# Three of the seven block products of Q and K split once more into seven quarter products, with the extra sums on GpSimd

## The chip, the cores and the metric

One core of a Trainium2 chip. The time is the device time of that core in microseconds (us), the median of several executions. A change of under 2% counts as "within 2%". The record marks each run as fast or slow by its time and by the clock that TensorE was granted.

## The reference, cut to what matters

Two attention blocks over x of 8 images x 512 channels x 1024 positions, all in fp32: group norm, one 1x1 convolution to Q, K and V, attention with 8 heads of 64, a projection, and the residual.

```python
xt = xn.reshape(B, C_, N)
qkv = jnp.einsum('oc,bcn->bon', qkv_w, xt) + qkv_b[None, :, None]
q, k, v = jnp.split(qkv, 3, axis=1)
...
attn = jax.nn.softmax(attn, axis=-1)
out = jnp.einsum('bhij,bhdj->bhdi', attn, v)
out = jnp.einsum('oc,bcn->bon', proj_w, out) + proj_b[None, :, None]
```

Q for one image is a 512x512 matrix times a 512x1024 matrix, K likewise. I call one image in one layer a *unit*; there are 16, worked off one after the other.

## The kernel before

The kernel already computes Q, K, V and the projection O with seven block products in place of eight: both matrices are cut 2x2, sums of blocks are multiplied, and the products are added up again. The three tiles `bx`, `by`, `bz` in PSUM, the memory into which this kernel's matmuls write, hold them; each is of two banks. To *evict* a tile is to read it out of PSUM into SBUF, the working memory; a product that is needed twice is copied out (`p1`) or added (`u2`, `u3`) while the tile goes on.

```python
def blocks(name, left, right, tokens, c11, others, done, u3_in):
    bx, by, bz = apair[0], sbank[0], apair[1]
    ...                                  # products(bank, k, start, stop): block product k
    products(bx, 1, True, False)
    p1 = work(accpool, "acc", "p1")
    nc.scalar.copy(p1, bx)
    done(sums)
    products(by, 6, True, False)
    u2 = work(trpool, "tr", "u2")
    nc.vector.tensor_add(u2, by, p1)
    done(sums)
    products(bx, 2, False, True)
    c11(bx)                              # ScalarE evicts it
    done(sums)
    products(by, 7, False, False)
    u3 = work(*u3_in, "u3")
    nc.vector.tensor_add(u3, by, p1)
    done(sums)
    products(bz, 5, True, False)
    others(1, 1, bz, u3)                 # VectorE evicts it and adds u3
    done(sums)
    products(by, 4, False, True)
    others(1, 0, by, p1)
    done(sums)
    products(bz, 3, False, True)
    others(0, 1, bz, u2)
    done(sums)
```

`done` counts the products of Q (1 to 7), K (8 to 14) and V (15 to 21) and at given numbers issues work left over from the attention of the unit before:

```python
def divide_last():
    divide(CC - 1)                       # VectorE: two SBUF inputs, 128x1024
    for h in range(NH):
        add_bias(CC - 1, h)              # ScalarE: two, each waits for the division
...
return {4: [lambda: reciprocals(CC - 1)], 10: [divide_last], 12: mixing[:2], 14: mixing[2:]}
```

## Time and profile before

| | us |
|---|---|
| median | 3341.2 |
| Q and K of a unit | 48.17 |
| V | 24.17 |
| O of the unit before | 24.13 |
| attention | 110.26 |

The stages of the fourth unit are the stretches of this view of the kernel before. Its columns are the stretch, its length, and for each engine the busy time with the count of instructions, then the granted TensorE clock (1.00 is all of it), the DMA share and GB/s.

```profile
core 0: us, PE busy (x) PEld busy (x) DVE busy (x) ACT busy (x) POOL busy (x), PEclk, DMA share, GB/s
618.20:666.37 48.17, 48.17 (x115) 21.38 (x114) 24.91 (x34) 7.59 (x11) 0.00 (x0) 1.00 0.14 45
666.37:690.54 24.17, 24.17 (x113) 21.28 (x112) 8.58 (x8) 2.02 (x2) 0.00 (x0) 1.00 0.07 22
690.54:714.67 24.13, 24.13 (x58) 10.45 (x56) 15.39 (x21) 1.01 (x1) 0.00 (x0) 1.00 0.41 153
714.67:824.93 110.26, 110.26 (x1034) 49.96 (x1033) 99.10 (x123) 76.59 (x83) 1.98 (x1) 1.00 0.08 21
```

TensorE is busy for the whole of each stretch. The others have room in Q and K (VectorE 24.9 of 48.2), and VectorE has little in attention (99.1 of 110.3).

### The profile page before, as it was taken

The page shows a single profiled execution, that of the slowest core. Times are in us where ns is not written, and L with a number is a line of the kernel's source. Part 1 is how long each engine was busy: PE and PEld are TensorE (multiplying, and loading weights), DVE is VectorE, ACT ScalarE, POOL GpSimd, SP SyncE. Part 2 cuts the span into 40 slices and gives each one's busy share as a digit, 9 for nine tenths or more (in the row PEclk, how much of TensorE's full clock was granted, in tenths as well). Part 3 has the DMA queues.
Part 4 walks back from the last instruction along what each step waited for, and adds up shares of the span by engine and source line. Part 5 has one row for each costly group of instructions (what it writes and reads, how often), then busy time and mean ns, then how long its engine had stood idle before and what let it go on. Part 6 is the DMA issues. An engine that isn't in the chain of part 4 may idle for free.

```text
span 3340.0 us, 51079 instructions
## 1 busy us (share of the span) xinstructions
PE 3315.5 (99%) x21002; PEld 1645.3 (49%) x21002; DVE 2375.6 (71%) x2977; ACT 1393.5 (42%) x1549; POOL 48.1 (1%) x32
## 2 busy tenths in 40 slices
PE   8999999999999999999999999999999999999999
PEld 4445454454544545455554544545445454454533
DVE  4876948769486684867848678585785957859577
ACT  1542706336063360733617235172451724517144
POOL 0000000000000000002000000000000000000000
PEclk9999999999999999999999999999999999999999
DMA  2011010110101102012020111201111011110121
GB/s 78 33 39 58 21 64 27 39 58 22 70 27 33 58 21 76 21 33 96 21 85 25 33 58 28 76 15 33 64 33 64 15 37 60 33 63 15 39 71 47
DMA packets 66844, 149.27 MB, mean 45 GB/s; under 512 B 20784, under 2 KB 21040, under 8 KB 66608
## 3 DMA queue, kind: packets, MB, share of 16 engines
q1 hardware_dynamic: 66608, 145.95, 13.3%
q8 instruction: 169, 2.77, 0.4%
q14 instruction: 67, 0.55, 0.1%
HBM read 110.26 MB, written 34.08 MB: 43 GB/s over the span
## 4 chain that ended last, share of the span: by engine, by line
PE 98%; DVE 1%; issue 0%; DMA 0%; ACT 0%; POOL 0%; SPq 0%; DVEq 0%
PE a L514 26%; PE a L288 26%; PE s L486 25%; PE s L288 19%; PE a L486 1%; PE s L437 0%; PE a L437 0%; DMA xn<-x_dram 0%; DVE acc L533 0%; DVE x L422 0%; DVE stats L184 0%; PE a L196 0%; DVE tr L546 0%; DVE u_o L390 0%; POOL y L216 0%
## 5 line engine op out<-in xcount | busy, mean ns | idle before, releaser
L494 ACT ACTIVATE p<-s 128x1024 f32<-128x1024 f32 x976 | 997.2, 1023 | 816.7 <-PE s L486 761.7
L514 PE MATMUL a<-p,v 64*64 64x512 f32 x8192 | 1101.2, 589 | 0.1
L486 PE MATMUL s<-q,k 64*64 64x512 f32 x7808 | 1059.3, 590 | 1.4 <-DVE v L375 1.4
L533 DVE TENSOR_TENSOR acc<-acc,p 128x1024 f32<-128x1024 f32 x768 | 938.7, 1222 | 88.8 <-ACT p L494 41.4
L514 PEld LDWEIGHTS a<-p,v 64*64 64x64 f32 x8192 | 384.9, 131 | 494.4 <-ACT p L494 349.6
L486 PEld LDWEIGHTS s<-q,k 64*64 64x64 f32 x7808 | 385.8, 133 | 437.1 <-issue 434.6
L288 PE MATMUL a<-xn,w 128*128 128x512 f32 x512 | 234.4, 601 | 4.0 <-DVE xn L244 4.0
L531 DVE TENSOR_TENSOR acc<-p,p 128x1024 f32<-128x1024 f32 x128 | 153.7, 1201 | 12.9 <-ACT p L494 12.9
L288 PEld LDWEIGHTS a<-xn,w 128*128 128x128 f32 x512 | 96.9, 192 | 132.7 <-issue 128.1
L546 DVE STREAM_TRANSPOSE tr<-acc 128x1024 f32<-128x1024 f32 x128 | 158.0, 1234 | 0.0
L556 DVE TENSOR_REDUCE red<-tr 128x32 f32<-128x1024 f32 x128 | 153.9, 1202 | 0.6
L540 DVE TENSOR_TENSOR ao<-a,tmp 128x512 f32<-128x512 f32 x128 | 88.0, 687 | 69.9 <-ACT tmp L539 69.9
L300 ACT COPY p_k<-a 128x1024 f32<-128x1024 f32 x16 | 16.2, 1012 | 255.1 <-PE a L288 255.1
L300 ACT COPY p_o<-a 128x1024 f32<-128x1024 f32 x15 | 15.2, 1012 | 244.2 <-PE a L288 244.2
L288 PE MATMUL a<-w,xn 128*128 128x256 f32 x512 | 115.7, 379 | 0.0
L288 PE MATMUL s<-xn,w 128*128 128x512 f32 x256 | 115.2, 593 | 0.4 <-DVE u_q L304 0.4
L300 ACT COPY p_v<-a 128x1024 f32<-128x1024 f32 x16 | 16.2, 1012 | 237.3 <-PE a L288 221.4
L288 PE MATMUL s<-x_t,s2w 128*128 128x512 f32 x256 | 115.1, 592 | 0.0
L288 PE MATMUL a<-x_t,s1w 128*128 128x512 f32 x256 | 115.1, 592 | 0.0
L288 PE MATMUL s<-x_t,w 128*128 128x512 f32 x256 | 115.1, 592 | 0.0
L288 PE MATMUL a<-xn,s4w 128*128 128x512 f32 x256 | 115.1, 592 | 0.0
L288 PE MATMUL a<-ao,wproj_wproj 128*128 128x512 f32 x240 | 107.9, 592 | 0.0
(129 smaller groups left out, 2843.4 us busy)
## 6 DMA issues: line engine op xcount, KB each, us to landing
rb<-drec SPq DMA_DIRECT2D x128, 256.0 KB, 3.9
xn<-mid SPq DMA_DIRECT2D x36, 512.0 KB, 5.0
xn<-x_dram SPq DMA_DIRECT2D x32, 512.0 KB, 5.1
x<-x_dram SPq DMA_DIRECT2D x32, 512.0 KB, 4.6
mid<-x SPq DMA_DIRECT2D x64, 256.0 KB, 2.1
x<-mid SPq DMA_DIRECT2D x28, 512.0 KB, 4.6
out_dram<-x SPq DMA_DIRECT2D x56, 256.0 KB, 2.1
w<-qkv_wT_dram SPq DMA_DIRECT2D x6, 1024.0 KB, 11.2
```

The costliest lines, as they stand in the source:

```text
L288: nc.tensor.matmul(dst, at[:, c, ts(i, P)], moving[:, c, :], start=start and c == 0 and not (tokens and i % 2), stop=stop and c == 1, skip ...
L300: nc.scalar.copy(p1, bx)
L486: nc.tensor.matmul(bank[e * H : (e + 1) * H, j, :], w.k[pr][j * H : (j + 1) * H, t * P + e * H : t * P + (e + 1) * H], w.q[pr][j * H : (j ...
L494: exp = nc.scalar.activation(p, bank, AF.Exp, scale=SCALE)
L514: nc.tensor.matmul(banks[r][j * H : (j + 1) * H, :], w.v[rows, t, lo : lo + D], p[rows, j, :], start=(t == 0), stop=(t == NT - 1),)
L531: nc.vector.tensor_add(acc, state["first"], p)
L533: nc.vector.tensor_add(acc, acc, p)
L540: i1 = nc.vector.tensor_add(w.ao[pr // 2][:, pr % 2, ts(qh, FD)], banks[1], tmp)
L546: nc.vector.transpose(tr, state["acc"].pop(c))
L556: nc.vector.tensor_reduce(red[:, :, qh, :], state["tr"].rearrange("p j (f i) -> p j f i", i=BL), AX.X, ALU.add)
```

## The change

The intent: split products 2, 4 and 3 of Q and of K once more, so that each takes seven calls of 128x128 on 256 columns. Before it took four on 512 columns (3.43 us from start to start in the kernel before), which last as long as eight on 256 (3.45 us in its V). The price is more sums. ScalarE copies the partial results out, GpSimd adds them, and GpSimd also makes the mixed quarter blocks. The quarter blocks of the weights are mixed once a layer, in its first unit. To make room in SBUF, the accumulator of attention and the transpose buffer go from two buffers to one. The diff, cut to its core:

```diff
-    accpool = pool("accpool", 2)
+    accpool = pool("accpool", 1)
-    trpool = pool("trpool", 2)
+    trpool = pool("trpool", 1)
+    def mix_inner(name, right):              # four GpSimd adds of 256 columns, for 2, 4 and 3
+        t = ppool.tile([P, 4, FD2], F32, tag="p", name=f"{name}_t")
+        ...
+        def inner_products(k, bank, more):
+            left, right = inner[k]
+            one, two = sbank[1][:, 0, :FD2], (bz if k == 2 else bx)[:, 0, :FD2]
+            product(1, one, True, False)
+            nc.scalar.copy(rest[:, 0, :FD2], one)
+            product(2, bank[:, 0, :FD2], False, True)
+            product(3, bank[:, 0, FD2:], False, True)
+            product(6, one, False, False)
+            nc.scalar.copy(rest[:, 0, FD2:], one)
+            product(4, bank[:, 1, :FD2], False, True)
+            product(5, two, True, True)
+            nc.scalar.copy(rest[:, 1, FD2:], two)
+            nc.gpsimd.tensor_add(rest[:, 0, FD2:], rest[:, 0, FD2:], rest[:, 1, FD2:])
+            product(7, one, False, True)
+            nc.scalar.copy(rest[:, 1, :FD2], one)
+            nc.gpsimd.tensor_add(rest[:, 1, FD2:], rest[:, 1, :FD2], rest[:, 1, FD2:])
+            if more is not None:
+                nc.gpsimd.tensor_add(more, more, rest)
-        products(bx, 2, False, True)
-        c11(bx)
+            c11(bx, inner_products(2, bx, None))     # now on VectorE, as the others are
-        products(by, 4, False, True)
+            inner_products(4, by, p1)
-        products(bz, 3, False, True)
+            inner_products(3, bz, u2)
-        return {4: [...], 10: [divide_last], 12: mixing[:2], 14: mixing[2:]}
+        return {4: [...], 9: [divide_last], 15: [partial(mix, 0)], 17: [partial(mix, 1)]}
```

I call the products inside a quartered product its *parts*, 1 to 7.

More of the change, by code (lines that the diff above doesn't have):

```diff
@@ L165, in mix_right, with mix_inner_left @@
         return {1: b11, 2: b21, 3: b22, 4: t4, 5: t1, 6: t2, 7: b12}, parts
+    INNER = (2, 4, 3)
+    def mix_inner(name, right):
+        gp = nc.gpsimd
+        b11, b12 = right[:, 0, :FD2], right[:, 0, FD2:]
+        b21, b22 = right[:, 1, :FD2], right[:, 1, FD2:]
+        t = ppool.tile([P, 4, FD2], F32, tag="p", name=f"{name}_t")
+        t1, t2, t3, t4 = (t[:, i, :] for i in range(4))
+        parts = [
+            partial(gp.tensor_sub, t1, b12, b11), partial(gp.tensor_sub, t2, b22, t1),
+            partial(gp.tensor_sub, t3, b22, b12), partial(gp.tensor_sub, t4, b21, t2),
+        ]
+        return {1: b11, 2: b21, 3: b22, 4: t4, 5: t1, 6: t2, 7: t3}, parts
+    def mix_inner_left(name, tag, left):
+        gp = nc.gpsimd
+        a11, a12 = left[:, 0, :P], left[:, 1, :P]
+        a21, a22 = left[:, 0, P:], left[:, 1, P:]
+        t = wpool.tile([P, 3, P], F32, tag=tag, name=name)
+        s1, s2, s4 = (t[:, i, :] for i in range(3))
+        parts = [
+            partial(gp.tensor_add, s1, a21, a22), partial(gp.tensor_sub, s2, s1, a11),
+            partial(gp.tensor_sub, a21, a11, a21), partial(gp.tensor_sub, s4, a12, s2),
+        ]
+        return {1: a11, 2: a12, 3: s4, 4: a22, 5: s1, 6: s2, 7: a21}, parts
     def load_proj(l, tag):
@@ L269, in fast_path, with blocks @@
         pass
-    def blocks(name, left, right, tokens, c11, others, done, u3_in):
+    def blocks(name, left, right, tokens, c11, others, done, u3_in, inner=None):
         bx, by, bz = apair[0], sbank[0], apair[1]
@@ L292, in products, with product @@
                     )
+        def inner_products(k, bank, more):
+            left, right = inner[k]
+            one, two = sbank[1][:, 0, :FD2], (bz if k == 2 else bx)[:, 0, :FD2]
+            rest = tpool.tile([P, 2, FD], F32, tag=f"o{k if k != 3 else 1}", name=f"m{k}_{name}")
+            def product(j, dst, start, stop):
+                nc.tensor.matmul(
+                    dst, left[j], right[j], start=start, stop=stop, skip_group_check=True
+                )
+            product(1, one, True, False)
[13 more added lines that the diff above has]
+                nc.gpsimd.tensor_add(more, more, rest)
+            return rest
         def work(pool, tag, k):
@@ L305, in blocks @@
         done(sums)
-        products(bx, 2, False, True)
-        c11(bx)
+        if inner:
+            c11(bx, inner_products(2, bx, None))
+        else:
+            products(bx, 2, False, True)
+            c11(bx)
         done(sums)
@@ L315, in blocks @@
         done(sums)
-        products(by, 4, False, True)
+        if inner:
+            inner_products(4, by, p1)
+        else:
+            products(by, 4, False, True)
         others(1, 0, by, p1)
         done(sums)
-        products(bz, 3, False, True)
+        if inner:
+            inner_products(3, bz, u2)
+        else:
+            products(bz, 3, False, True)
         others(0, 1, bz, u2)
@@ L340, in projections, with c11 @@
             ]
-            def c11(bank):
-                for i in range(2):
-                    w.last[sel].append(
-                        nc.scalar.activation(
-                            tiles[i][:, :FD], bank[:, i, :], AF.Identity,
-                            bias=vec[:, l, bias, i : i + 1],
-                        )
-                    )
+            def c11(bank, more):
+                others(0, 0, bank, more)
             def others(r, h, bank, more):
@@ L361, in projections @@
             left = w.lefts["qk".index(sel)]
-            blocks(f"{sel}_{u}", left, w.right, False, c11, others, done, (ppool, "p"))
+            blocks(f"{sel}_{u}", left, w.right, False, c11, others, done, (ppool, "p"), w.inner[sel])
             setattr(w, sel, tiles)
@@ L642, in divide_last, with mix @@
                 add_bias(CC - 1, h)
-        w.right_o, mixing = mix_right(f"o_{u}", *w.ao)
-        return {4: [lambda: reciprocals(CC - 1)], 10: [divide_last], 12: mixing[:2], 14: mixing[2:]}
+        mixing = []
+        def mix(i):
+            if not mixing:
+                w.right_o, parts = mix_right(f"o_{u}", *w.ao)
+                mixing.extend(parts)
+            for part in mixing[2 * i : 2 * i + 2]:
+                part()
+        return {
+            4: [lambda: reciprocals(CC - 1)], 9: [divide_last], 15: [partial(mix, 0)],
+            17: [partial(mix, 1)],
+        }
     xn = load_xn(0)
@@ L661, in fast_path @@
     rest[12] = mixing_o
+    inner_left = {}
     old = None
@@ L670, in fast_path @@
         if u == B + 1:
-            rest[16] = mixing_o
+            rest[18] = mixing_o
+        inner_right, inner_parts = {}, {"q": [], "k": []}
+        for k in INNER:
+            if u % B == 0:
+                for i, sel in enumerate("qk"):
+                    inner_left[sel, k], parts = mix_inner_left(
+                        f"l{k}{sel}_{u}", f"l{k}{sel}", lefts[i][k]
+                    )
+                    inner_parts[sel] += parts
+            inner_right[k], parts = mix_inner(f"r{k}_{u}", right[k])
+            inner_parts["q"] += parts
+        w.inner = {
+            sel: {k: (inner_left[sel, k], inner_right[k]) for k in INNER} for sel in "qk"
+        }
+        for g, sel in ((1 if u == 0 else 0, "q"), (7, "k")):
+            rest[g] = [*rest.get(g, ()), *inner_parts[sel]]
+        for part in rest.get(0, ()):
+            part()
         projections(w, rest)
@@ L742, in verdict @@
         nc.vector.tensor_mul(both, low[:, 0:1], low[:, 1:2])
-    project_last(old, [part for g in (4, 10) for part in rest[g]] + [verdict])
+    project_last(old, [part for g in (4, 9) for part in rest[g]] + [verdict])
     nc.tensor.matmul(turns[0][:1, :1], both, ones[:, :1], start=True, stop=True)
```

## The prediction

> **What bounds the kernel now.** I read the page first: busy shares, slices, chain.
>
> ```profile
> PE 3315.5 (99%) x21002; PEld 1645.3 (49%) x21002; DVE 2375.6 (71%) x2977; ACT 1393.5 (42%) x1549; POOL 48.1 (1%) x32
> PE 98%; DVE 1%; issue 0%; DMA 0%; ACT 0%; POOL 0%; SPq 0%; DVEq 0%
> ```
>
> TensorE is busy 99% and is 98% of the chain that ended last; the first slice alone is not full. So each us of matmul removed is a us of the kernel, and each us that TensorE is made to wait is a us lost: nothing absorbs it. GpSimd is idle.
>
> Second, the timeline of one unit (one image in one layer; 16 of them, 206.7 us apart). At the start of Q, TensorE, then ScalarE, then VectorE:
>
> ```profile
> 411.46 3.70 PE L288 MATMUL a<-xn,w 128*128 128x512 f32 x8
> 415.00 3.60 PE L288 MATMUL s<-x_t,s2w 128*128 128x512 f32 x8
> 418.44 3.60 PE L288 MATMUL a<-xn,w 128*128 128x512 f32 x8
> ...
> 415.20 1.01 ACT L300 COPY p_q<-a 128x1024 f32<-128x1024 f32 x1 [1.79 <-PE a L288]
> ...
> 411.91 2.55 DVE L533 TENSOR_TENSOR acc<-acc,p 128x1024 f32<-128x1024 f32 x2
> 414.38 0.68 DVE L540 TENSOR_TENSOR ao<-a,tmp 128x512 f32<-128x512 f32 x1
> 414.98 1.23 DVE L546 STREAM_TRANSPOSE tr<-acc 128x1024 f32<-128x1024 f32 x1
> 416.25 1.22 DVE L556 TENSOR_REDUCE red<-tr 128x32 f32<-128x1024 f32 x1
> 417.39 1.22 DVE L669 TENSOR_TENSOR x_t<-xn,x_t 128x1024 f32<-128x1024 f32 x1
> 418.52 1.22 DVE L669 TENSOR_TENSOR xn<-xn 128x1024 f32<-128x1024 f32 x1
> 419.65 1.22 DVE L304 TENSOR_TENSOR u_q<-s,p_q 128x1024 f32<-128x1024 f32 x1
> ```
>
> A block product starts every 3.43 us: four calls of 128x512, each two records (x8). VectorE comes out of attention backlogged, with no gap; u_q ends at 420.9, and the product that overwrites its bank is due at 421.87: one us of slack.
>
> Third, V, whose calls have the 256 columns that the change will use, and the middle of K:
>
> ```profile
> 459.64 3.62 PE L288 MATMUL a<-w,xn 128*128 128x256 f32 x16
> 463.09 3.62 PE L288 MATMUL s<-s2w,x_t 128*128 128x256 f32 x16
> ...
> 463.34 1.01 ACT L300 COPY p_v<-a 128x1024 f32<-128x1024 f32 x1 [14.76 <-PE a L288]
> ...
> 442.74 1.23 DVE L304 TENSOR_TENSOR u_k<-s,p_k 128x1024 f32<-128x1024 f32 x1 [5.53 <-PE s L288]
> 443.88 1.22 DVE L596 SCALAR_TENSOR_TENSOR ao<-ao,rb 128x1024 f32<-128x1024 f32 x1
> 445.02 0.08 DVE L596 DVE_READ_ACCUMULATOR ao<-ao,rb 128x1 f32 x1
> 446.10 1.26 ACT L345 ACTIVATE k<-a,vec 128x512 f32<-128x512 f32 x2 [5.86 <-PE a L288]
> 447.26 1.33 ACT L603 ACTIVATE ao<-ao,vec 128x512 f32<-128x512 f32 x2
> ```
>
> Eight 256-column calls also take 3.45 us, so one takes 0.43. The copy starts 0.25 us after the next product has begun. Then, for how fast TensorE resumes after a wait, the start of attention, and for GpSimd beside VectorE the one place where both work:
>
> ```profile
> 508.04 1.29 DVE L422 TENSOR_TENSOR x<-a,u_o 128x512 f32<-128x512 f32 x2 [0.95 <-PE a L288]
> 509.45 0.41 PEld L486 LDWEIGHTS a<-q,k 64*64 64x64 f32 x8 [0.45 <-DVE x L422]
> 509.70 1.04 PE L486 MATMUL a<-q,k 64*64 64x512 f32 x8
> ...
> 1531.00 1.27 POOL L688 TENSOR_TENSOR w<-w 128x512 f32<-128x512 f32 x1
> 1532.23 1.26 POOL L688 TENSOR_TENSOR s4w<-w,s2w 128x512 f32<-128x512 f32 x1
> ...
> 1532.66 3.05 DVE L390 SCALAR_TENSOR_TENSOR u_o<-x,vec,u_o 128x512 f32<-128x512 f32 x2
> ```
>
> The wait sits on the weight load: read done at 509.33, load at 509.45, matmul at 509.70, so 0.37 us from the reader's end to the matmul.
>
> [...]
> 1. [...] The trace has 1.23 us between starts for 512. [...]
> 2. [...] the pair above took 3.05 us beside GpSimd, 1.41 elsewhere, 0.8 more for each.
> [...]
>
> **The change part by part.**
> Removed: each of products 2, 4, 3 of Q and K becomes seven calls of 256 columns in place of eight. Saved 0.43 us, times 6 a unit, 2.57 us; times 16, **41 us**. That is all there is to gain, 1.2%.
>
> Added on the path: inside a quartered product one PSUM area holds parts 1, 1+6 and 1+6+7, and ScalarE copies it between. A copy of 128x256: from 0.58 us for 512 columns and 1.01 for 1024, 0.84 ns a column, so 0.37. A round trip from the end of a matmul to the next one in that area: 0.23 + 0.37 + 0.37 = 0.97 us.
> - Parts 6 and 7 each have two calls, 0.86 us, ahead of them as cover: 0.11 short, 12 times a unit, 1.3 us.
> - Product 3 follows product 4 at once, and its part 1 overwrites the area that part 7 of product 4 has just filled: no cover. 0.97 us, twice a unit, 1.9.
> - The block after (K, then V) begins in the bank that held part 5 of product 3; only part 7 (0.43) covers it: 0.54, twice, 1.1.
>
> Together **4.3 us a unit**, already more than the 2.57 saved.
>
> Moved: the last division and its two bias adds go from after K's product 2 to before it. ScalarE then holds the two bias adds ahead of the copies that K's product 2 needs, and they wait for the division. On the times above: product 6 of K ends at 442.47; u_k, then the division until 445.1; biases 445.2 to 446.5; small copy until 446.9; matmul at 447.2. It was due 1.29 us (three calls) after 442.47, at 443.8. **3.4 us a unit**, in 15 units.
>
> Start of a unit: twelve GpSimd adds of 256 columns[...]. The first four meet VectorE's last sums and the division, two SBUF inputs each: at some 0.5 us (the 0.8 scaled to the shorter adds) for three, VectorE is 1.5 us late, u_q ends near 422.5. TensorE would want the bank at 421.4 plus the waits above; I count 1.0. With one accumulator buffer, p_q can't be copied before the transpose is done (417.7), so it ends at 418.8 in place of 416.2, just when product 2 needs the bank: 0.4. The other eight adds wait for x_t, near 420.1,[...]; the parts of Q's product 2 queue behind them[...]. Sum **2.3 us a unit**, the softest term.
>
> Off the path: [...] VectorE takes over two evictions of 0.75 from ScalarE. The single transpose buffer costs nothing[...]. Moving the mixing into V costs nothing; V's VectorE has gaps of 2 to 5 us.
>
> Sum for 14 ordinary units: 4.3 + 3.4 + 2.3 - 2.6 = 7.4, 104 us. First unit: no division, about 4. First unit of layer 1: also 24 adds of 128 columns, twelve ahead of Q's[...]. Total +119: 3341.9 + 119, about **3460 us**.
>
> **The rivals.**
> - *All waits hidden*: TensorE shows only the 41 us, 3301. For it: [...] GpSimd idles. Against: the round trip in one PSUM area is three durations from the trace with no cover in two places a unit.
> - *Round trips only*: bias adds and start of unit cost nothing, because something orders ScalarE otherwise than I read. Then 3342 + 16 x 1.7, 3369, within 2%. Against: in K above the bias adds keep program order.
> - *GpSimd becomes the bound*: if small adds carry a large fixed cost (say 1.2 us for 256), each partial sum comes 3 us later and its evictions hold VectorE; products 4 of Q and K then wait too, 3 us more a unit and above 3500. For it: only one size was measured; its power op on 128x4 takes 1.98.
> - *The buffers bind*: the single accumulator delays the copy by far more than 0.4. Then the start costs 4 or 5 us, 3500.
>
> **Range and chances.** The firm part, 4.3 + 3.4 - 2.6, gives +78 or so, 3420; dropping a third of each gives 3395. The soft terms doubled give 3500. 8 in 10: 3395 to 3505. Slower by over 2% means above 3408.7, which the firm part alone passes: 0.80. Within 2%: 0.17, if the bias adds do not block. Faster by over 2%: 0.03, since more than the 41 us would have to come.
>
> **What would show it.** Busy time of TensorE's Q and K groups lower by 41 us; 128x256 copies near 0.37 us; weight loads in the new products waiting for ScalarE's copies, near 1 us at product 3, near 3.4 at K's product 2; the bias adds ahead of K's small copies; sums at a unit's start above 1.22 us[...]. Wrong would be a unit spacing under 208.4 us, or waits mostly for GpSimd.

Cut from it are a list with a length for GpSimd's adds of 256 columns, which no trace of this case had shown, and what rests on that length. Two terms of the sum are among this: the last of three at a unit's start (0.9 us, beside the 1.0 and 0.4 that still stand; together the 2.3), and 4 us in the first unit of layer 1. The sum, +119 us and 3460, has both in it; without them it comes to about +101 (119 less 16 times 0.9 and less 4), 3442. The firm part, +78, does not contain them.

What is left of the list is from the rows above it: GpSimd's adds of 512 columns start 1.23 us apart, and VectorE's pair beside them took 3.05 us where it takes 1.41 elsewhere. The 0.5 us for the shorter adds is my estimate from the 0.8 of that pair. That ScalarE keeps the order of the program is read from K: the division ends at 445.10 and ScalarE is idle until 446.10, and yet the bias adds come after the eviction that starts there, at 447.26.

## The result, and the profile after

| | before | after |
|---|---|---|
| median, us | 3341.2 (6 runs) | 3432.7 (6 runs) |
| Q and K, all units | 774.0 | 861.6 |
| V, all units | 388.2 | 390.0 |
| O | 361.9 | 361.9 |
| attention | 1765.0 | 1766.8 |

The ratio is 1.0278 (95% interval 1.0265 to 1.0292): slower. Ratios here are the mean time of one kernel's fast runs over that of the other's fast runs of the same rounds, so they are not quite the ratio of the medians. The stages are told from the starts of the matmuls in the two traces. Nearly all of the 91.5 us came into Q and K.

The page of the kernel after, busy shares and the chain that ended last by engine:

```profile
PE 3324.7 (97%) x21578; PEld 1798.3 (52%) x21578; DVE 2449.6 (71%) x3041; ACT 1497.8 (44%) x1869; POOL 565.5 (16%) x528
...
PE 80%; DVE 9%; issue 6%; POOL 3%; ACT 2%; DMA 0%; DVEq 0%; POOLq 0%; SPq 0%; ACTq 0%
```

TensorE is no longer the whole chain: a fifth of it runs through VectorE, GpSimd, ScalarE and issue. That is a chain followed back from the end, not time lost; much of it ran beside matmuls. Its busy time is up, 3324.7 us from 3315.5, although it has less to do. Matmuls held at half their clock are a part of this, and not the larger: the first stretch below has the full clock (1.00), and its busy time is 47.67 us where e11, the last experiment, with the waits gone, has 45.70. Around each wait some 0.16 us of the last call's modelled end (0.59 us, where the next call follows at 0.43) and 0.11 us of a slower first call (0.70 us in place of 0.59) count as busy too. The same four stretches of the fourth unit as above:

```profile
637.13:689.63 52.50, 47.67 (x150) 27.44 (x148) 25.66 (x34) 13.72 (x30) 25.45 (x25) 1.00 0.11 31
689.63:713.91 24.28, 24.28 (x113) 21.43 (x113) 12.25 (x12) 2.40 (x3) 4.00 (x4) 1.00 0.14 44
713.91:738.03 24.12, 24.12 (x57) 10.48 (x55) 15.39 (x21) 1.01 (x1) 0.00 (x0) 1.00 0.41 153
738.03:848.41 110.38, 110.38 (x1033) 53.34 (x1032) 99.15 (x123) 76.52 (x83) 3.65 (x2) 1.00 0.07 21
```

Q and K take 52.50 us in place of 48.17, and TensorE is idle for 4.83 of them. Who held it is in the view of waits, here of the weight loads of TensorE, at which this trace shows its waits: us in all, times, longest.

```profile
PEld s L331 <- ACT m_k L336: 48.7, 15, 3.4
...
PEld s L331 <- DVE u_q L372: 17.9, 16, 5.5
PEld s L317 <- DVE u_q L362: 16.5, 15, 1.1
...
PEld s L331 <- ACT m_q L346: 14.1, 16, 1.2
PEld s L331 <- ACT m_k L346: 13.8, 16, 0.9
...
PEld a L317 <- ACT m_q L343: 6.9, 16, 0.4
PEld a L317 <- ACT m_k L343: 6.9, 16, 0.4
PEld a L331 <- ACT p_q L358: 6.8, 15, 2.2
```

In the timeline of that unit the weight loads are idle 0.24 us between matmuls of 512 columns with no wait (0.19 us of load in each 0.43), so a row can be too large by some 0.2 us for each time. I took the loss from the starts of the matmuls: how much later one begins than 0.215 us (256 columns) or 0.429 us (512) after the one before. Those sums are what is quoted from here on.

The largest, in K of the fourth unit. TensorE, then ScalarE, then VectorE in the timeline of the kernel after:

```profile
670.53 0.60 PE L331 MATMUL a<-xn,l2k 128*128 128x256 f32 x2
673.97 0.70 PE L331 MATMUL s<-r_t,l2k 128*128 128x256 f32 x2 [2.84 <-ACT m_k L336]
...
672.33 1.33 ACT L664 ACTIVATE ao<-ao,vec 128x512 f32<-128x512 f32 x2 [4.83 <-DVE ao L657]
673.57 0.35 ACT L336 COPY m_k<-s 128x256 f32<-128x256 f32 x1
...
669.93 1.22 DVE L362 TENSOR_TENSOR u_k<-s,p_k 128x1024 f32<-128x1024 f32 x1 [1.64 <-PE s L317]
671.07 1.22 DVE L657 SCALAR_TENSOR_TENSOR ao<-ao,rb 128x1024 f32<-128x1024 f32 x1
```

Part 6 of K's product 2 needs ScalarE's copy of part 1 (`m_k`). The copy stands behind the two bias adds, these wait for the division, and the division for `u_k`. TensorE stands still for 3.0 us, in 15 units.

And the end of Q in the same timeline, product 4 into product 3 (the same line 331 for all parts):

```profile
658.32 0.59 PE L331 MATMUL s<-r_t,w 128*128 128x256 f32 x2
659.38 0.70 PE L331 MATMUL s<-xn,s4w 128*128 128x256 f32 x2 [0.46 <-ACT m_q L346]
...
658.96 0.37 ACT L346 COPY m_q<-s 128x256 f32<-128x256 f32 x1
```

Part 1 of product 3 overwrites what part 7 of product 4 left, so it starts only when that is copied: 0.05 us after the copy's end, and 0.63 late.

### The profile page after: what moved, and what is told of

Read it like the earlier page. It is cut to its first block, busy times and chain, and to the rows that moved or that the text cites. A ratio compares the mean times of both kernels' runs of the same rounds, so it can differ in the third digit from the quotient of the medians.

```text
span 3431.1 us, 53597 instructions
## 1 busy us (share of the span) xinstructions
PE 3324.7 (97%) x21578; PEld 1798.3 (52%) x21578; DVE 2449.6 (71%) x3041; ACT 1497.8 (44%) x1869; POOL 565.5 (16%) x528
## 3 DMA queue, kind: packets, MB, share of 16 engines
HBM read 110.26 MB, written 34.08 MB: 42 GB/s over the span
## 4 chain that ended last, share of the span: by engine, by line
PE 80%; DVE 9%; issue 6%; POOL 3%; ACT 2%; DMA 0%; DVEq 0%; POOLq 0%; SPq 0%; ACTq 0%
PE s L547 21%; PE a L575 21%; PE a L317 16%; PE s L317 13%; DVE acc L594 5%; PE s L331 5%; PE a L331 3%; POOL r_t L762 2%; PE a L547 1%; DVE ao L657 1%; DVE tr L607 1%; ACT ao L664 1%; DVE u_q L372 1%; DVE acc L592 1%; ACT p L555 1%
## 5 line engine op out<-in xcount | busy, mean ns | idle before, releaser
L575 PE MATMUL a<-p,v 64*64 64x512 f32 x8192 | 1116.2, 589 | 0.1
L547 PE MATMUL s<-q,k 64*64 64x512 f32 x7808 | 1074.7, 590 | 1.4 <-DVE v L436 1.4
L575 PEld LDWEIGHTS a<-p,v 64*64 64x64 f32 x8192 | 400.0, 132 | 479.2 <-ACT p L555 338.8
L547 PEld LDWEIGHTS s<-q,k 64*64 64x64 f32 x7808 | 415.6, 133 | 407.7 <-issue 405.2
L762 POOL TENSOR_TENSOR r_t<-xn 128x256 f32<-128x256 f32 x60 | 74.0, 1233 | 1196.7 <-PE a L575 1196.7
L244 POOL TENSOR_TENSOR y<-var,half 128x4 f32<-128x4 f32 x16 | 32.2, 2015 | 1006.1 <-DVE var L242 1006.1
L664 ACT ACTIVATE ao<-ao,vec 128x512 f32<-128x512 f32 x128 | 88.3, 713 | 98.6 <-DVE ao L657 98.6
L317 PE MATMUL a<-xn,w 128*128 128x512 f32 x256 | 120.2, 613 | 4.8 <-DVE xn L272 4.4
L317 PEld LDWEIGHTS a<-w,xn 128*128 128x128 f32 x512 | 96.1, 190 | 19.1 <-ACT m_k L343 6.9
L266 ACT ACTIVATE xn<-xn,shift,scale 128x512 f32<-128x512 f32 x124 | 99.5, 805 | 7.1 <-DVE shift L262 7.1
```

Of the source, the lines that this page charges most:

```text
L266: nc.scalar.activation(cols, cols, AF.Identity, bias=st["shift"][:, c : c + 1], scale=st["scale"][:, c : c + 1],)
L317: nc.tensor.matmul(dst, at[:, c, ts(i, P)], moving[:, c, :], start=start and c == 0 and not (tokens and i % 2), stop=stop and c == 1, skip ...
L547: nc.tensor.matmul(bank[e * H : (e + 1) * H, j, :], w.k[pr][j * H : (j + 1) * H, t * P + e * H : t * P + (e + 1) * H], w.q[pr][j * H : (j ...
L575: nc.tensor.matmul(banks[r][j * H : (j + 1) * H, :], w.v[rows, t, lo : lo + D], p[rows, j, :], start=(t == 0), stop=(t == NT - 1),)
L664: nc.scalar.activation(cols, cols, AF.Identity, bias=vec[:, units[u][0], VB, pr : pr + 1])
L762: part()
```

## The experiments

Eleven kernels ran. The first four are the changed kernel with one thing undone or altered, and the old kernel with one part of the change; their rounds shared the runs of the kernel before, 3341 us.

**1. The bias adds after product 2.** The division stays at 9.

```diff
-            divide(CC - 1)
-            for h in range(NH):
-                add_bias(CC - 1, h)
+            divide(CC - 1)
+        def bias_last():
+            for h in range(NH):
+                add_bias(CC - 1, h)
-            4: [...], 9: [divide_last], 15: ...
+            4: [...], 9: [divide_last], 10: [bias_last], 15: ...
```

> The changed kernel with one thing moved: the two bias adds that follow the last division are issued after K's product 2 and not before it (the division itself stays). My theory ([...] the bias adds hold the small copies that K's quartered product 2 needs): the wait of 3.0 us, 15 times, goes, 45 us, and with it most of the stretches in which TensorE was granted half its clock, some 8 more: 3380 us. Rival (GpSimd's sums set the pace of K): nothing moves, 3433.

Measured: 3373.2 us, ratio 1.0098 (1.0081 to 1.0114). The change loses 59.5 of its 91.5 us by the place of two instructions. The wait of 3.0 us is gone from the trace, and so is every stretch at half the clock except those at the start and the end (granted clock of the profiled run 0.998, in the change 0.994). The rival falls.

**2. Other PSUM areas, first try.** Product 3's partial sums go to the second bank of the score tile.

```diff
             one, two = sbank[1][:, 0, :FD2], (bz if k == 2 else bx)[:, 0, :FD2]
+            if k == 3:
+                one, two = sbank[1][:, 1, :FD2], sbank[1][:, 0, :FD2]
```

> The changed kernel with other PSUM areas for product 3: its partial sums go to the second bank of the pair and its part 5 to the first, so that nothing is overwritten that ScalarE is about to copy. My theory (round trips through one area): the waits between product 4 and product 3 (24 us in the trace) and before the next block (8 us) go: 3401 us. Rival (product 3 waits for GpSimd or for its evictions): under 5 us gained.

Measured: 3464.7 us, ratio 1.0369 (1.0352 to 1.0386), slower than the change itself. Both theories missed, because the edit did not do what it was meant to. TensorE and ScalarE in the timeline of this kernel:

```profile
663.73 0.59 PE L333 MATMUL s<-r_t,w 128*128 128x256 f32 x2
664.78 0.70 PE L333 MATMUL s<-xn,s4w 128*128 128x256 f32 x2 [0.46 <-ACT m_q L348]
...
667.24 0.70 PE L333 MATMUL s<-r_t,l3q 128*128 128x256 f32 x2
668.40 0.70 PE L333 MATMUL s<-r_t,s4w 128*128 128x256 f32 x2 [0.46 <-ACT m_q L345]
...
664.36 0.37 ACT L348 COPY m_q<-s 128x256 f32<-128x256 f32 x1
...
667.98 0.37 ACT L345 COPY m_q<-s 128x256 f32<-128x256 f32 x1 [0.79 <-PE s L333]
```

The matmul at 664.78 now writes the other bank and still waits for the copy that ends at 664.73. And part 7 (668.40) waits for the copy of part 5 (ends 668.35), which is in the other bank too: a new wait of 0.63 us, 32 times. The dependences of this program are kept for the two-bank tile as a whole. Of the round trips, only the wait before the next block (0.30 us) is gone from this trace, because part 5 is no longer in that block's bank. For the wait into product 3 the run neither supports nor refutes the theory; experiment 5 does it properly.

**3. Eight of the twelve GpSimd adds later.** The mixed quarter blocks for products 4 and 3 are made after product 2's sums.

```diff
-            inner_parts["q"] += parts
+            if k == 2:
+                inner_parts["q"] += parts
+            else:
+                later += parts
...
+        rest[3] = [*later, *rest.get(3, ())]
```

> The changed kernel with the eight GpSimd adds for products 4 and 3 of a unit issued after product 2's sums in place of before them. My theory (product 2's sums queue behind twelve adds, so Q's second sum u3 is late and product 4 waits for it): the 16 us of that wait go, those of the first units of both layers too: 3417 us. Rival (the adds are needed where they were; late ones make products 4 and 3 wait): slower than 3433.

Measured: 3424.2 us, ratio 1.0253 (1.0236 to 1.0270). Q's product 4 no longer waits for `u_q`: the 16 us are gone from the trace. The time fell by only 8.5, because this kernel's trace has more stretches at half the clock, 13 of 3.4 us between start and end in place of 8 (granted clock of the profiled run 0.993, in the change 0.994). They follow the wait in K, which is still there. (What such a stretch costs is under "right or wrong" below.)

**4. The old kernel with the single buffers.** Only the two pool sizes.

> The kernel before with only the single buffers for the accumulator and the transpose. My theory ([...] only the first copy of Q waits for the transpose, about 1 us, and that is covered): 3341 to 3344 us. Rival (the single buffer is what makes the start of a unit wait): 10 us or more slower.

Measured: 3343.3 us, ratio 1.0007 (0.9990 to 1.0024). Single buffers by themselves cost nothing in the time that can be told from noise. In the trace the attention of an ordinary unit takes 110.38 us, as in the change, where the kernel before has 110.26: most of the change's 2 us in attention come from here. They can still matter where something else is late, which the next ones show.

**5. Other PSUM areas, second try.** Product 4 and product 3 use two different tiles in turn, and part 5 comes third, so that its copy is long done when its area is needed.

```diff
-            one, two = sbank[1][:, 0, :FD2], (bz if k == 2 else bx)[:, 0, :FD2]
+            one, two = {2: (sbank[1], bz), 4: (bx, sbank[1]), 3: (sbank[1], bx)}[k]
+            one, two = one[:, 0, :FD2], two[:, 0, :FD2]
             product(1, ...); product(2, ...)
+            product(5, two, True, True)
+            nc.scalar.copy(rest[:, 1, FD2:], two)
             product(6, ...); product(3, ...); product(4, ...)
-            product(5, two, True, True)
-            nc.scalar.copy(rest[:, 1, FD2:], two)
             product(7, ...)
```

> The second try at the PSUM areas. The first put both areas into the two banks of one tile, and every wait there was for the tile as a whole, so it tested nothing but added waits. Now product 4 keeps its partial sums in the first tile (bx) and its part 5 in the score tile, product 3 the other way round, and part 5 comes third. My theory (round trips through one area): the waits between product 4 and product 3 (20 and 3.4 us) and before the next block (6.2 and 1.7) go, 31 us: 3401 us. Rival (product 3 waits for evictions or for GpSimd anyway): under 5 us gained.

Measured: 3403.1 us, ratio 1.0186 (1.0169 to 1.0203; whether over 2% is unclear), 29.6 us faster than the change. The waits into product 3 and into the next block are not in its trace any more. The theory of the round trips holds.

**6. No GpSimd adds at a unit's start.** The quarter products take unmixed blocks.

```diff
-        return {1: b11, 2: b21, 3: b22, 4: t4, 5: t1, 6: t2, 7: t3}, parts
+        return {1: b11, 2: b21, 3: b22, 4: b21, 5: b12, 6: b22, 7: b11}, []
```

> The changed kernel without the twelve GpSimd adds of a unit's start; the quarter products take unmixed blocks, so the result is wrong on purpose, with the same matmuls and copies. My theory (those adds read SBUF beside VectorE's two-input instructions and delay them, and the sums of product 2 queue behind them): VectorE's division and last sums are back at 1.22 us, the waits for u_q (13.7 and 4.0), for p_q (4.8) and for Q's u3 (16) go, some 36 us: 3397 us. Rival 1 (only the queue on GpSimd matters[...]): 16 us, 3417. Rival 2 (the single buffers are what makes the start wait): nothing at the start moves, 3417 too, with u_q and p_q waiting as before.

Measured: 10858 us, and the result correct. The wrong Q and K failed the kernel's own check of its sums, so that after its fast part the program ran its general path, which computes all again. The whole time says nothing, but the trace holds the fast part, which ends at 3399.0 us with the matmul that makes the flag (3424.8 in the change). That is 26 us, not the 36 expected; this trace also has more stretches at half the clock in its middle, 13 in place of 8. In it the waits for `p_q` and for Q's `u3` are gone, and of `u_q`'s wait one is left. VectorE and TensorE at the start of the fourth unit:

```profile
629.18 1.23 DVE L594 TENSOR_TENSOR acc<-acc,p 128x1024 f32<-128x1024 f32 x1
...
635.59 1.22 DVE L362 TENSOR_TENSOR u_q<-s,p_q 128x1024 f32<-128x1024 f32 x1
...
637.18 3.60 PE L317 MATMUL s<-xn,w 128*128 128x512 f32 x8
```

The last sum takes 1.23 us; in the change two of them take 3.40. `u_q` is ready at 636.81, before the product that needs its bank. The single buffers are still single here, so rival 2 falls, and rival 1 too, since more than the queue went away.

**7. Three edits together** (1, 3 and 5).

> The changed kernel with three of the edits at once: bias adds after product 2, the new areas and order of parts, the adds for products 4 and 3 after product 2's sums. If the waits are independent: 3373 - 31 - 15 = 3327 us, with the waits for u_q and p_q at a unit's start left, some 20 us. Rival (removing one wait brings out another of about the same size, since VectorE and GpSimd are the real limit of Q and K): 3350 or more, slower than the kernel before.

Measured: 3323.9 us, ratio 0.9949 (0.9932 to 0.9965). The waits are independent ones: none came up in place of those removed, and 3433 is now 3324. Alone, the three edits gained 59.5, 29.6 and 8.5 us, 98 together; the other 11 us go with the stretches at half the clock, which e3 and e5 still had (granted clock 0.993 and 0.994) and this trace has only at the start and the end (1.000). The kernel is half a per cent faster than the one before, which is within 2%. What is left in its trace is the start of a unit: 13.7 and 1.7 us for `u_q`, 3.2 and 1.6 for `p_q`. Product 3 now follows product 4 without a gap (TensorE, fourth unit):

```profile
635.98 0.59 PE L332 MATMUL a<-r_t,w 128*128 128x256 f32 x2
636.41 0.59 PE L332 MATMUL s<-xn,s4w 128*128 128x256 f32 x2
```

**8. In addition, two of VectorE's four mixing instructions earlier.**

```diff
-        for part in mixing[2:]:
+        for part in mixing[2 if u == 0 else 4 :]:
...
-            elif c == 2 + CC and t in (2, 5):
-                mixing[int(t == 5)]()
+            elif c == 2 + CC and t in (2, 5, 6, 7):
+                mixing[(2, 5, 6, 7).index(t)]()
```

> e7 with the last two of VectorE's four mixing instructions moved from a unit's start into the attention before it. My theory: VectorE has 2.3 us less of backlog when Q begins, so neither u_q nor p_q makes TensorE wait: 3310 us, about 1% faster than the kernel before, 3301 being the limit of the saved matmuls. Rival (VectorE is full in attention, so the two push the exponentials out): attention longer by over 1 us a unit and no gain over e7.

Measured: 3342.1 us, ratio 1.0005 (0.9988 to 1.0021). My theory was right on Q and K and wrong on the sum: Q and K fell from 46.87 to 45.99 us a unit, and attention rose from 110.38 to 112.38. The rival holds. ScalarE in this kernel's attention:

```profile
614.10 1.94 ACT L556 ACTIVATE p<-s 128x1024 f32<-128x1024 f32 x2 [2.95 <-DVE acc L593]
```

The exponential waits 2.95 us for VectorE's sum, which frees its buffer. TensorE in turn waits for such an exponential 14 times, 24.6 us in all. VectorE at 90% had no 2.3 us to spare there.

**9. Unused tiles to shift the buffers.** Two tiles are taken from the pool and never touched, so that the first mixed block would get the buffer of a later exponential and GpSimd would start later.

```diff
+        for i in range(2):
+            ppool.tile([P, N], F32, tag="p", name=f"skip{i}_{u}")
```

> e7 with two unused tiles taken from the pool first, so that the first GpSimd tile of a unit gets the buffer of the last but one exponential and its four adds can start only when VectorE is done with all but its last sum. My theory (the four adds hold up VectorE's division and sums, each by some 0.5 us, and nothing else): division and sums back at 1.22 us, the waits for u_q (13.7 and 1.7) and p_q (3.2 and 1.6) gone, 20 us: 3304 us, 1.1% faster than the kernel before. Rival (the adds are then too late for product 2's third part): no gain over e7, 3324, with a wait for GpSimd in its place.

Measured: 3324.0 us, ratio 0.9948 (0.9934 to 0.9962), the same as e7. The edit did not take: GpSimd's first add of the fourth unit starts at 613.68 us, and at 613.76 in e7. It seems that tiles which nobody touches took no buffer. Nothing is learned about the theory.

**10. Division and bias adds both behind product 2, as in the kernel before.**

```diff
-            4: [...], 9: [divide_last], 15: ...
+            4: [...], 10: [divide_last], 15: ...
```

> The changed kernel with the division and its bias adds both back behind product 2, as in the kernel before. My theory: as e1, 3373 us, since VectorE has slack there. Rival (the division was moved because behind product 2's evictions, which wait for GpSimd, it makes u_k late): slower than e1 by 10 us or more, with a wait for u_k.

Measured: 3374.6 us, ratio 1.0099 (1.0084 to 1.0115), as e1. Leaving `divide_last` where the kernel before has it would have been right; K's `u_k` shows no wait. ScalarE in K of the fourth unit, where the small copy now goes ahead of the bias adds:

```profile
663.02 0.37 ACT L336 COPY m_k<-s 128x256 f32<-128x256 f32 x1 [2.81 <-PE s L331]
...
669.12 1.33 ACT L664 ACTIVATE ao<-ao,vec 128x512 f32<-128x512 f32 x2 [3.14 <-DVE ao L657]
```

**11. GpSimd's first add after VectorE's last sum.** The edit that e9 meant, as a dependence.

```diff
-                nc.vector.tensor_add(acc, acc, p)
+                w.last_sum = nc.vector.tensor_add(acc, acc, p)
...
+            n = part()
+            if i == 0 and old is not None:
+                tc.add_manual_dep(getattr(n, "ins", n), name_of(old.last_sum), DEP, reason="after the sums")
```

> e7 with the first GpSimd add of a unit made to depend on VectorE's last sum of the attention (e9's unused tiles changed nothing: they took no buffer, and the adds began where they did in e7). Expected as for e9: division and last sums back at 1.22 us, the waits for u_q (13.7 and 1.7) and p_q (3.2 and 1.6) gone, 20 us: 3304 us, 1.1% faster than the kernel before. Rival: the adds are then too late for product 2's third part, and a wait for GpSimd takes the place, 3324.

Measured: 3306.7 us, ratio 0.9894 (0.9878 to 0.9911): 1.1% faster than the kernel before, which is within 2%, with an interval that leaves out 1. It does the same work as the change, with 126 us less. The start of the fourth unit in the kernel after, VectorE and GpSimd:

```profile
636.64 1.75 DVE L657 SCALAR_TENSOR_TENSOR ao<-ao,rb 128x1024 f32<-128x1024 f32 x1
...
638.32 3.40 DVE L594 TENSOR_TENSOR acc<-acc,p 128x1024 f32<-128x1024 f32 x2
...
635.53 1.78 POOL L762 TENSOR_TENSOR r_t<-xn 128x256 f32<-128x256 f32 x1 [80.83 <-PE a L575]
637.39 1.59 POOL L762 TENSOR_TENSOR r_t<-xn,r_t 128x256 f32<-128x256 f32 x1
```

and in e11:

```profile
611.23 1.22 DVE L658 SCALAR_TENSOR_TENSOR ao<-ao,rb 128x1024 f32<-128x1024 f32 x1
...
612.37 2.55 DVE L595 TENSOR_TENSOR acc<-acc,p 128x1024 f32<-128x1024 f32 x2
...
615.06 0.72 POOL L769 TENSOR_TENSOR r_t<-xn 128x256 f32<-128x256 f32 x1 [85.77 <-DVE acc L595]
615.86 0.73 POOL L769 TENSOR_TENSOR r_t<-xn,r_t 128x256 f32<-128x256 f32 x1
```

Beside each other, the division takes 1.75 us in place of 1.22, two sums 3.40 in place of 2.55, and GpSimd's adds over twice their time. One after the other, both are back at their own, and GpSimd, started 3.8 us after the division's start in place of 1.1 before it, has its four adds done 6.7 us after the division's start in place of 5.7. So the delay costs it about one us, and that one us was free but in one unit, the ninth, where TensorE waited 0.7 us for such an add.

## Why the prediction was right or wrong

It was right in direction and size: slower, 3460 forecast and 3432.7 measured, inside the range. Of the +119 us forecast, +91.5 came. Term by term, all units together; the measured ones are the late starts of matmuls in the trace of the kernel after:

| term | forecast, us | measured, us |
|---|---|---|
| matmuls saved | -41 | -40 |
| no cover for parts 6 and 7 | 21 | 0 |
| product 4 into product 3 | 31 | 24 |
| last part 5 before the next block | 17 | 10 |
| bias adds ahead of K's copies | 51 | 47 |
| start of a unit | 37 | 38 |
| TensorE at half its clock | not foreseen | 9 |
| sum, and the first units | 119 | 88 |

The forecasts are the per-unit terms times 16, or 15 for the bias adds; 14 of the 37 us at the start of a unit, and 4 us in the last line, are the terms cut. The last line has 3 us more for what I gave the first unit of each layer beyond them. The measured sum lacks 3 us, of which attention has 2. The 40 are from e11, where the waits are gone: a unit's Q and K take 45.70 us in place of 48.17, 2.47 times 16.

But for one term, the waits, the queues that hold them and the order of their sizes were as forecast. One of the signs asked for did not show: TensorE's busy time in Q and K of the fourth unit fell by 0.5 us, not by 2.6 (see the page above). e1 and e10 show the bias adds, e5 the two round trips, e3 the queue on GpSimd, e6 and e11 that GpSimd and VectorE hold each other up, and e7 that these are independent.

**The term that failed** is "Parts 6 and 7 each have two calls, 0.86 us, ahead of them as cover: 0.11 short, 12 times a unit, 1.3 us". In the trace the parts of a quartered product follow each other at 0.43 us with no wait. The round trip was mis-sized: I had put 0.37 us from the end of the reading to the next matmul, taken from the start of attention. In the timeline above, part 7 of product 4 starts at 658.32 and holds TensorE until 658.75, the copy runs from 658.96 to 659.33, and the matmul follows at 659.38; the second pass after it comes 0.11 late. That is 0.63 us and 0.11, together 0.74 in place of 0.97. With 0.63 the 0.86 us of cover is enough. The same error makes the next two rows too large: 0.74 in place of 0.97 between products 4 and 3, and 0.30 (0.195 and 0.106) in place of 0.54 before the next block. These three rows differ from the measured ones by 35 us, more than the whole of the error.

**The start of a unit** came out right in all, 38 us for 37, with its parts otherwise mixed: `u_q` 0.97 us (0.86 and 0.11) in 15 units where I had 1.0; `p_q` 0.3 us for 0.4; `u3` 16 us in the trace, of which 8 lie in the first unit of each layer, where twelve more GpSimd adds stand ahead. I had given 0.9 to each unit and 4 to one first unit, the two terms cut above; the other units have 0.57. The remaining 3 us are matmuls at half the clock after the `u3` waits of the two first units. That the sum came out so near is luck.

**What I had not foreseen** is the clock. After the 3.0 us pause in K, the trace has stretches of 3.4 us in which TensorE's granted clock was 0.50, in six of 15 units. The kernel after in the thirteenth unit, timeline of TensorE:

```profile
2584.53 1.22 PE L331 MATMUL s<-r_t,l2k 128*128 128x256 f32 x2 [2.84 <-ACT m_k L336]
2585.54 1.06 PE L331 MATMUL a<-r_t,w 128*128 128x256 f32 x2
2586.40 1.06 PE L331 MATMUL a<-r_t,l2k 128*128 128x256 f32 x2
2587.25 1.06 PE L331 MATMUL s<-r_t,w 128*128 128x256 f32 x2
```

Each row is one call of two passes. They should follow each other at 0.43 us, and they start 0.85 to 1.01 apart. Units with such a stretch after K's pause have Q and K of 53.9 to 55.5 us, where the others have 52.5; over five such units that is 9 us more (the sixth, at the start of layer 1, has other waits too). e1 and e10 have no such stretch in the middle of the program, which explains why e1 gained more than the 47 us of its wait.

Which pauses of the same 3.0 us were followed by one goes, in this trace, with where a pause lies in time. What follows is measured here, from the clock that the trace of the kernel after records and from its matmuls. All its stretches at half the clock begin on one grid of 3.413 us: the first after K's pause at 460.76 us, the next at 1307.27, 248 steps later, another at 2583.86, 622 steps after the first. In the interval 457.35 to 460.76 TensorE stood still for 2.50 us of its pause, and the granted clock was 0.50 from there to 464.17. The pause of the fourth unit was split by a line of the grid, 1.43 us on one side and 1.58 on the other, and the clock stayed at 1.00. The largest part that fell into one interval was 2.33 us or more in five of the 15 units, and half the clock followed in all five; 2.13 or less in eight, and it followed in none; 2.16 in two, and it followed in one of them. So what told these pauses apart was where they fell on the grid. 15 pauses of about one length show no more than that.

## What to carry to other kernels

Where TensorE is the whole chain (98% of it in the kernel before), fewer matmuls pay only if every round trip through another engine has other matmuls ahead of it. Here 0.86 us of them were enough for a round trip of 0.63, and with none TensorE was 0.63 us late: count the calls between a part and the next one in the same tile, and give neighbours different tiles. Before moving an instruction to an earlier place in a program, look at every queue that it passes through, and at what will stand behind it there: two bias adds held a copy, and TensorE for 3.0 us, in 15 units, and cost more here (47 us) than all the quartered products save (40). Work moved to an idle engine is not free where the two engines hold each other up, as GpSimd and VectorE did here (1.75 us in place of 1.22 for the division, 1.6 to 1.8 in place of 0.72 for GpSimd's adds); here it paid to start it when the neighbour's division and sums were done (e11, 17 us less than e7).
